# Graph-network layers on one Trainium2 core: sigmoid through tanh, attention scores spread through DRAM, first loads in another order

## The chip, the cores and the metric

The kernel runs on one core of a Trainium2 chip. The time is device time in microseconds (us), from one launch to its end. The profile has its own span, from the first to the last instruction, which is about 2 us shorter.

## What is computed

128 graphs of 128 nodes with 256 features each, and an adjacency matrix for every graph. Layer 0 is a gated graph network of three steps, layer 1 an attention over neighbours. Both work on a normalized input and add their result to `x`.

```python
def gru(inp, h):
    gi, gh = inp @ w_ih.T + b_ih, h @ w_hh.T + b_hh
    r, z = sigmoid(i_r + h_r), sigmoid(i_z + h_z)
    n = tanh(i_n + r * h_n)
    return (1 - z) * n + z * h
h = relu(layernorm(x))                       # layer 0
for i in range(3):
    m = h @ weight[i]
    aggr = einsum('bst,bsd->btd', A, m)      # A: adjacency as 0 and 1
    h = gru(aggr, h)
x = x + h
h = relu(layernorm(x))                       # layer 1
Wh = h @ W;  s = Wh.sum(-1)
e = leaky_relu(s[:, :, None] + s[:, None, :], 0.2)
alpha = softmax(where(adj == 0, -inf, e))
x = x + alpha @ Wh
```

## The kernel before

Four graphs make a group, so there are 32 groups. A group goes through three network steps (layers 0 to 2 in the code) and then through the attention. Three groups in different steps are worked on in turn, in an order that the list `turns` gives.

**The order of instructions.** The code does not issue its instructions as it goes. `op(engine, ns, fn, reads, writes, ...)` puts an operation on a list with an estimated duration, the buffers it uses and a due time. `Plan.run` then sorts all of them with these estimates and with a lag from one engine to the next, and issues them in that order; each engine, and SyncE (SP) for all transfers, works its own list off in sequence. An argument `two=True` tells the planner that a VectorE operation and a GpSimd operation can't run at once. So a changed estimate can change the order of everything. The matrix products of the gates carry due times of their own (`plan.cursor`), and form the chain around which the rest is placed.

**The gate products.** State and edge sums are multiplied with the two gate matrices in 2x2 blocks by seven products in place of eight, with sums and differences of blocks: `hs` (`node_sums` of the state, on GpSimd), `gs` (of the edge sums, on VectorE), `s_hh`, `s_x0` to `s_x2` (of the matrices, by `block_sums` at the start). The edge matrices `s_x` are compositions of `weight[i]` with `w_ih` (L431). `product` (L655, and L662 for the last step, which leaves its result with nodes on partitions) fills PSUM banks X, Y, Q for the gates r and z (`x_rz`, `y_rz`, `q_rz`) and for n (`x_n`, `y_n`, `q_n`). ScalarE copies X to Y (L702) and Y to `t2` and `t3` in SBUF (`put`, L692), VectorE adds Q (L695).

**The gates.** `gru` (steps 0 and 1) takes four blocks, from T3, X, Y and T2. For each it has the sigmoid of r and z on ScalarE (L740, L750), then on VectorE `(h_n + b) * r` (L743) and `+ i_n` (L747); for halves of the group it has tanh on ScalarE (L756) and three VectorE operations (L759 to L764) for `n + z * (h - n)`. `gru_rows` does the same for the last step (L778 to L804). The bias of n comes as a pointer to a column of `bias_h` in L743.

**Transposes.** Between node-wise and feature-wise layouts the data go through SP's transposing transfers, as 16-bit planes (`turned_halves`, `turned_parts`, `pl` to `plT`, L546). The edge sums (L597) multiply three bf16 parts of the state with the adjacency.

**Attention.** For a group: norm of `x1` to `h1`; `hw` (L868) gives the scores `s`, one number for each node; `turn_s` (L892) transposes the scores on TensorE into the PSUM bank `misc`, so that each partition has all 128 scores of a graph; the addition of these (L898) and of the own score (L899), leaky relu (L901), row maximum (L903), exponential (L910), sum (L912); transpose of the weights (`turned_weights`, L955, or by TensorE at L922 in the last two groups), weighted sum (L611), product with `W` (L935), and the addition to `x1` (L940), which is stored at L943. The exponential's estimate has 2570 ns more for loads of ScalarE's function table.

**Start.** SP's first entries in the kernel before are `w_ih` (768 KB, into `rz`), `x` of group 0, `w_hh` (768 KB), the message weights of layer 0, the adjacency, `x` of group 1, the two biases, `x` of group 2, the message weights of layer 1. `turned` (L344) transposes the gate weights on TensorE; the message weights follow at L418.

Of the kernel before, what the change touches and what calls it, by code (L numbers as in the profile page):

```python
# [23 lines left out]
MARGIN = 8000  # L24
GATES = 18150
# [185 lines left out]
def kernel(  # L211
# [31 lines left out]
    work = ctx.enter_context(tc.tile_pool(name="work", bufs=1))  # L243
    banks = ctx.enter_context(tc.tile_pool(name="banks", bufs=1, space=bass.MemoryType.PSUM))
# [25 lines left out]
        "hw": (1, "all", work, [P, D]), "e": (2, "all", work, [P, G, N]),  # L270
        "eT": (1, "all", work, [P, G, N]), "uT": (2, "all", work, [P, KD, GN]),
# [3 lines left out]
        "bias_s": (1, "all", const, [P, 3 * KD]),  # L275
# [37 lines left out]
    W = {t: buf(t) for t in ("s_hh", "s_x0", "s_x1", "s_x2", "bias_i", "bias_h", "bias_s", "seed_x",  # L313
# [12 lines left out]
    def load(dst, get, src, ns=100):  # L326
        op("SP", ns, lambda: nc.sync.dma_start(get(dst), src), [], [dst])
# [8 lines left out]
    def turned(src, dst, evict):  # L336

        for k in range(KD):
            for a in range(2):
                ps = bank()  # L340

                def turn(k=k, a=a, ps=ps):
                    for c in range(3):
                        nc.tensor.transpose(flat(ps)[:, c * P:(c + 1) * P],  # L344
                                            nat(src)[:, 3 * a + c, k * P:(k + 1) * P], ident)
                op("PE", 330, turn, [src], [ps])
                to_sbuf(evict[(2 * k + a) % len(evict)], 3 * P, ps, dst[k], 3 * P * a)
# [25 lines left out]
    def weights():  # L373
# [7 lines left out]
        def load_msg(layer):  # L381
            op("SP", 1300, lambda: nc.sync.dma_start(
                square(w_msg[layer]), weight[layer].rearrange("(k p) e -> p k e", p=P)),
               [], [w_msg[layer]])


        plan.due = -10 ** 6
        load(w_ih_nat, nat, w_ih.rearrange("(c p) e -> p c e", p=P), 4000)
        load_msg(0)
        plan.due = 10 ** 9  # L390
        load(w_hh_nat, nat, w_hh.rearrange("(c p) e -> p c e", p=P), 4000)
        load_msg(1)
        for t, src in (("bias_i", b_ih), ("bias_h", b_hh)):
            load(W[t], ap, src.rearrange("(c p) -> p c", p=P), 500)
        op("DVE", 170, lambda: nc.vector.tensor_add(ap(W["bias_s"]), ap(W["bias_i"]),
                                                    ap(W["bias_h"])),
           [W["bias_i"], W["bias_h"]], [W["bias_s"]])

# [44 lines left out]
        for t, i, b in ((tmp[0], 0, b_ih), (tmp[1], 0, b_hh), (tmp[2], 0, b_hh), (tmp[2], 1, b_ih)):  # L443
            n = t is tmp[2]
            op("SP", 500, lambda t=t, i=i, b=b, n=n: nc.sync.dma_start(
# [16 lines left out]
        load(W["w1"], ap, w_att.rearrange("(k p) e -> p k e", p=P), 1300)  # L462
# [209 lines left out]
    def products(layer, hT, hs, aT, gs, rows=False):  # L672
# [18 lines left out]
        def put(t, y):  # L691
            op("ACT", 590, lambda: nc.scalar.copy(ap(t), ap(y)), [y], [t])  # L692
# [4 lines left out]
        for kind, parts in kinds:  # L697
            X[kind], Y[kind] = buf("x_" + kind), buf("y_" + kind)
            if rows:
                seed(X[kind], kind, W["seed_x"])  # L700
            product(X[kind], 1, parts, not rows, rows=rows)
            op("ACT", 590, lambda x=X[kind], y=Y[kind]: nc.scalar.copy(ap(y), ap(x)),  # L702
               [X[kind]], [Y[kind]], mark=(plan.group, layer, kind))
# [5 lines left out]
        for kind, parts in kinds:  # L709
            product(Y[kind], 6, parts, False, rows=rows)  # L710
            T2[kind] = buf("t2_" + kind)
            put(T2[kind], Y[kind])
# [14 lines left out]
        return (1, 1, T3), (0, 0, X), y + (Y,), t2 + (T2,)  # L727

    def gru(layer, hT, hs, aT, gs):

        blocks = products(layer, hT, hs, aT, gs)
# [5 lines left out]
        for j, n, src in blocks:  # L737
# [3 lines left out]
                view(rz, 0)[:, j, n, :], ap(s_rz)[:, 0, :], AF.Sigmoid, bias=ap(W["bias_s"])[:, c:c + 1]),  # L741
               [s_rz, W["bias_s"]], [(rz, i, i + 1)])
            op("DVE", 480, lambda j=j, n=n, nn=nn, c=cn: nc.vector.scalar_tensor_tensor(  # L743
                view(u)[:, j, n, :], ap(nn)[:, 0, :], ap(W["bias_h"])[:, c:c + 1], view(rz, 0)[:, j, n, :],
                op0=OP.add, op1=OP.mult), [nn, (rz, i, i + 1), W["bias_h"]], [(u, i, i + 1)],
               two=nn.tag[0] == "t")
            op("DVE", 422, lambda j=j, n=n, nn=nn: nc.vector.tensor_tensor(  # L747
                view(u)[:, j, n, :], view(u)[:, j, n, :], ap(nn)[:, 1, :], OP.add),
               [nn], [(u, i, i + 1)], two=nn.tag[0] == "t")
            op("ACT", 500, lambda j=j, n=n, s_rz=s_rz, c=cz: nc.scalar.activation(  # L750
                view(rz, 1)[:, j, n, :], ap(s_rz)[:, 1, :], AF.Sigmoid, bias=ap(W["bias_s"])[:, c:c + 1]),
               [s_rz, W["bias_s"]], [(rz, 4 + i, 5 + i)])
        for j in (1, 0):
# [8 lines left out]
            op("DVE", 690, lambda d=d, cols=cols: nc.vector.tensor_tensor(  # L762
                ap(d), ap(d), ap(rz)[:, 1, cols], OP.mult), [(rz, 4 + lo, 4 + hi)], [d], two=True)
            op("DVE", 690, lambda j=j, d=d, cols=cols: nc.vector.tensor_tensor(  # L764
                ap(hT)[:, j, :], ap(u)[:, cols], ap(d), OP.add), [(u, lo, hi), d], [(hT, lo, hi)], two=True)

    def gru_rows(layer, hT, hs, aT, gs, rows, x1):

        blocks = products(layer, hT, hs, aT, gs, rows=True)
# [4 lines left out]
        for j, n, src in blocks:  # L774
# [5 lines left out]
                ap(s_rz).rearrange("p g (q m) -> p g q m", q=2), AF.Sigmoid),  # L780
               [s_rz], [(rz, i, i + 1), (rz, 4 + i, 5 + i)])
            op("DVE", 422, lambda outs=outs, graphs=graphs, nn=nn: nc.vector.tensor_tensor(
                view(u)[:, graphs, outs], ap(nn)[:, :, 0:P],
# [211 lines left out]
```

## Time and profile before

| | before |
|---|---|
| median of 3 runs | 2139.39 us (2138.39 to 2139.82) |
| the profiled execution | 2138.75 us, span 2136.9 us |
| TensorE matmul busy | 2108.1 us, 99% |
| VectorE busy | 1750.7 us, 82% |
| ScalarE busy | 1587.1 us, 74% |
| GpSimd busy | 951.0 us, 45% |
| transfers | 129.35 MB, queue busy 27.1% of 16 engines |

In lines of the profile, L12 is line 12 of the kernel before. PE is TensorE's matmuls, PEld its weight loads, DVE is VectorE, ACT is ScalarE, POOL is GpSimd, SPq is SyncE's queue. A group of instructions reads: line, engine, operation, output <- inputs, shapes, count, then busy us and mean ns of one, then idle time of the engine just before it and what ended that. A wait reads: who waited, for whom, us in total, times, longest. An engine that is busy less than the whole span costs time only where the engine that sets the end waits for it.

### The profile page before, as it was taken

Reading aid. Unit: us, or ns where it says so; the run is one execution under the profiler, and the core shown is the slowest. Engines: PE = TensorE matmul, PEld = TensorE weight load, DVE = VectorE, ACT = ScalarE, POOL = GpSimd, SP = SyncE. Lnnn points to the kernel's source line nnn. Section 1 sums busy time; section 2 is a strip of 40 time slices with the busy share of each in tenths; the row PEclk is TensorE's granted clock in tenths of the full one; section 3 lists DMA queues with packets and bytes.
Section 4 is the critical chain, followed back from the end, with each engine's and each line's share of the span. In section 5 each row is a group of like instructions: output and inputs, shape, how many; then the busy total and the mean of one; then the engine's idle time right before and its main releaser. Section 6 shows DMA issues by size and latency. Waiting matters only on the chain.

```text
span 2136.9 us, 33989 instructions
## 1 busy us (share of the span) xinstructions
PE 2108.1 (99%) x12550; PEld 1879.9 (88%) x12550; DVE 1750.7 (82%) x3297; ACT 1587.1 (74%) x2705; POOL 951.0 (45%) x889
## 2 busy tenths in 40 slices
PE   8999999999999999999999999999999999999997
PEld 7889888898888988889988889888888988988886
DVE  5677878788888889888898788888889888778777
ACT  5567877777877877777877777777777888676774
POOL 5545453445544445544344544355444454335421
PEclk9999999999999999999999999999999999999998
DMA  4222223232242312332222231313223323222221
GB/s 143 45 50 50 45 50 89 45 77 48 45 89 60 75 37 49 79 70 65 55 62 56 68 75 40 94 32 69 65 51 84 46 38 82 50 46 37 59 68 35
DMA packets 333430, 129.35 MB, mean 61 GB/s; under 512 B 264656, under 2 KB 333008, under 8 KB 333264
## 3 DMA queue, kind: packets, MB, share of 16 engines
q1 hardware_dynamic: 333264, 127.18, 27.1%
q8 instruction: 99, 1.62, 0.3%
q14 instruction: 67, 0.55, 0.1%
HBM read 45.36 MB, written 16.78 MB: 29 GB/s over the span
## 4 chain that ended last, share of the span: by engine, by line
PE 94%; DVE 3%; ACT 1%; DMA 1%; issue 1%; SPq 0%; DVEq 0%; ACTq 0%
PE y_rz L655 15%; PE q_rz L655 10%; PE x_rz L655 10%; PE y_rz L662 8%; PE y_n L655 7%; PE misc L597 6%; PE q_rz L662 5%; PE x_n L655 5%; PE x_rz L662 5%; PE q_n L655 5%; PE misc L935 5%; PE y_n L662 4%; PE misc L611 3%; PE x_n L662 3%; PE q_n L662 3%; PE misc L892 1%
## 5 line engine op out<-in xcount | busy, mean ns | idle before, releaser
L692 ACT COPY t_rz<-y_rz 128x512 f32<-128x512 f32 x192 | 112.3, 585 | 200.5 <-PE y_rz L662 104.9
L557 POOL TENSOR_TENSOR r<-rows 128x512 f32<-128x512 f32 x128 | 148.2, 1177 | 221.1 <-ACT rows L540 121.6
L625 POOL TENSOR_TENSOR hs<-hT 128x512 f32<-128x512 f32 x96 | 131.3, 1368 | 183.7 <-PE y_n L662 126.7
L655 PE MATMUL y_rz<-hs,s_hh 128*128 128x256 f32 x768 | 198.0, 380 | 2.6 <-ACT t_rz L692 2.6
L655 PE MATMUL y_rz<-gs,s_x 128*128 128x256 f32 x768 | 197.1, 379 | 0.0
L695 DVE TENSOR_TENSOR t_rz<-t_rz,q_rz 128x512 f32<-128x512 f32 x192 | 131.3, 684 | 69.4 <-PE q_rz L662 26.0
L582 POOL TENSOR_TENSOR pl<-d,pl 128x512 bf16<-128x512 f32 x64 | 77.9, 1219 | 217.8 <-ACT pl L580 217.7
L560 POOL TENSOR_TENSOR p<-r 128x512 bf16<-128x512 f32 x128 | 168.1, 1332 | 0.0
L655 PEld LDWEIGHTS y_rz<-gs,s_x 128*128 128x128 f32 x768 | 146.0, 190 | 19.8
L655 PEld LDWEIGHTS y_rz<-hs,s_hh 128*128 128x128 f32 x768 | 141.5, 190 | 21.8 <-ACT t_rz L692 4.0
L799 POOL TENSOR_TENSOR x<-x,u 128x512 f32<-128x512 f32 x64 | 88.1, 1379 | 143.0 <-ACT u L795 140.1
L695 DVE TENSOR_TENSOR t_n<-t_n,q_n 128x512 f32<-128x512 f32 x192 | 131.3, 684 | 22.5 <-ACT t_n L692 8.5
L629 POOL TENSOR_TENSOR hs<-hT,hs 128x256 f32<-128x256 f32 x96 | 74.1, 773 | 149.4 <-PE q_n L662 130.7
L577 POOL TENSOR_TENSOR d<-hT,pl 128x512 f32<-128x512 f32 x64 | 77.9, 1221 | 131.6 <-ACT pl L575 125.9
L692 ACT COPY t_n<-y_n 128x512 f32<-128x512 f32 x192 | 112.1, 584 | 29.5 <-PE y_n L655 16.8
L655 PE MATMUL x_rz<-hT,s_hh 128*128 128x256 f32 x512 | 131.5, 379 | 0.0
L655 PE MATMUL x_rz<-aT,s_x 128*128 128x256 f32 x512 | 131.5, 379 | 0.0
L935 PE MATMUL misc<-w,uT 128*128 128x256 f32 x512 | 121.7, 383 | 3.1 <-DVE e L898 1.7
L600 ACT COPY aT<-misc 128x512 f32<-128x512 f32 x192 | 110.6, 584 | 19.1 <-PE misc L597 13.7
L625 DVE TENSOR_TENSOR gs<-aT 128x512 f32<-128x512 f32 x96 | 96.8, 1009 | 27.4 <-ACT aT L600 27.4
L759 DVE TENSOR_TENSOR d<-hT,u 128x512 f32<-128x512 f32 x128 | 106.0, 828 | 12.2 <-ACT u L756 12.1
L655 PE MATMUL y_n<-hs,s_hh 128*128 128x256 f32 x384 | 114.5, 380 | 0.0
(215 smaller groups left out, 6548.9 us busy)
## 6 DMA issues: line engine op xcount, KB each, us to landing
rows<-in_x_dram SPq DMA_DIRECT2D x32, 512.0 KB, 4.2
x<-in_x_dram SPq DMA_DIRECT2D x32, 512.0 KB, 4.1
out_dram<-x SPq DMA_DIRECT2D x31, 512.0 KB, 3.0
at<-in_adj_dram SPq DMA_DIRECT2D x32, 256.0 KB, 2.8
plT<-pl SPq DMA_TRANSPOSE x186, 3.6
rz<-in_L_gnn_w_ih_dram SPq DMA_DIRECT2D x1, 768.0 KB, 5.0
rz<-in_L_gnn_w_hh_dram SPq DMA_DIRECT2D x1, 768.0 KB, 7.7
e<-in_L_gnn_weight_dram SPq DMA_DIRECT2D x3, 256.0 KB, 8.0
```

The lines of the kernel that those rows point to most:

```text
L557: op("POOL", 1106, lambda part=part: nc.gpsimd.tensor_tensor(ap(r1)[:, part], ap(rows)[:, part], top(rows)[:, part], OP.subtract), [(rows, ...
L560: op("POOL", 1050, lambda part=part: nc.gpsimd.tensor_tensor(ap(p3)[:, part], ap(r1)[:, part], top(r1)[:, part], OP.subtract), [(r1, n, n ...
L597: nc.tensor.matmul(flat(ps)[:, b * N:(b + 1) * N], part(i, b, k), ap(a)[:, b, :], start=(i == 0), stop=(i == 2))
L600: op("ACT", 590, lambda k=k, ps=ps: nc.scalar.copy(ap(dst)[:, k, :], flat(ps)), [ps], [(dst, 2 * k, 2 * k + 2)])
L625: op(eng, cost, lambda: sub(ap(w)[:, 0:2, :], blocks()[:, 1::2, :], blocks()[:, 0:2, :], OP.subtract), [t], [(w, 0, 2)], two=True)
L655: nc.tensor.matmul(ap(bank)[:, half, :], ap(w)[:, i - 1, q, :], source(t, sums), start=(first and c == 0 and m == 0), stop=False, skip_gro ...
L662: nc.tensor.matmul(ap(bank)[:, m, half * P:(half + len(chunk)) * P], source(t, sums)[:, m * N:(m + 1) * N], ap(w)[:, i - 1, q:q + len(chun ...
L692: op("ACT", 590, lambda: nc.scalar.copy(ap(t), ap(y)), [y], [t])
L695: op("DVE", 690, lambda: nc.vector.tensor_tensor(ap(t), ap(t), ap(q), OP.add), [q], [t])
L759: op("DVE", 690, lambda j=j, d=d, cols=cols: nc.vector.tensor_tensor(ap(d), ap(hT)[:, j, :], ap(u)[:, cols], OP.subtract), [(hT, lo, hi), ...
L799: op("POOL", 1290, lambda cols=cols, part=part: nc.gpsimd.tensor_tensor(part(x1), part(x1), ap(u)[:, cols], OP.add), [(u, lo, hi)], [(x1, ...
L935: nc.tensor.matmul(ap(ps)[:, b, :], ap(uT)[:, k, (m + b) * N:(m + b + 1) * N], ap(w1)[:, k, :], start=(k == 0), stop=(k == KD - 1))
```

## The change

1. `sigmoid(v)` is written as `(tanh(v / 2) + 1) / 2`. The activation becomes `Tanh` with scale 0.5 and a halved bias sum. The `+ 1` and the factor 0.5 go into the VectorE operations after it, which become scalar_tensor_tensor. For the block from X, which has r times a sum with a pointer bias, one more VectorE operation adds the 1. For the other blocks the bias of n is added by ScalarE when it copies: `put` copies in two halves, the first with a bias, for X to Y and for Y to T2 of kind n in steps 0 and 1. The exponential's estimate loses its 2570 ns.
2. For groups 0 to 29 the scores go to a DRAM tile `s_out` with one transfer (`128x4x1`, elements of 4 bytes) and come back with a second one that gives every partition all scores (`s_all`, 128x512). The planner takes 9500 and 5200 ns until they are there. The last two groups keep the transposes.
3. Loads get an estimate from their size (3 ns for a KB) and a lag of 3300 ns. `w_ih` is loaded in two halves; `turned` does the first half of rows first and waits for that half alone. The message weights of layers 0 and 1 get earlier due times. SP's first entries become: two halves of `w_ih`, message weights of layers 0 and 1, `x` of group 0, `w_hh`, adjacency, `x` of group 1, the biases, `x` of group 2.

```diff
+KB = 3
...
-    def load(dst, get, src, ns=100):
-        op("SP", ns, lambda: nc.sync.dma_start(get(dst), src), [], [dst])
+    def load(dst, get, src, kb):
+        op("SP", kb * KB, lambda: nc.sync.dma_start(get(dst), src), [], [dst], lag=3300)
...
-        for k in range(KD):
-            for a in range(2):
+        for a in range(2):
+            for k in range(KD):
...
-                op("PE", 330, turn, [src], [ps])
+                op("PE", 330, turn, [(src, a, a + 1)], [ps])
...
-        plan.due = -10 ** 6
-        load(w_ih_nat, nat, w_ih.rearrange("(c p) e -> p c e", p=P), 4000)
+        plan.due = -10 ** 9
+        for a in range(2):
+            part = slice(3 * a, 3 * a + 3)
+            op("SP", 384 * KB, lambda part=part: nc.sync.dma_start(
+                nat(w_ih_nat)[:, part], w_ih.rearrange("(c p) e -> p c e", p=P)[:, part]),
+               [], [(w_ih_nat, a, a + 1)], lag=3300)
         load_msg(0)
         plan.due = 10 ** 9
-        load(w_hh_nat, nat, w_hh.rearrange("(c p) e -> p c e", p=P), 4000)
+        load(w_hh_nat, nat, w_hh.rearrange("(c p) e -> p c e", p=P), 768)
+        plan.due = -10 ** 8
         load_msg(1)
+        plan.due = 10 ** 9
...
-        def put(t, y):
-            op("ACT", 590, lambda: nc.scalar.copy(ap(t), ap(y)), [y], [t])
+        def put(t, y, bias=None, mark=None):
+            if bias is None or rows:
+                op("ACT", 590, lambda: nc.scalar.copy(ap(t), ap(y)), [y], [t], mark=mark)
+                return
+            def halves():
+                nc.scalar.activation(ap(t)[:, 0], ap(y)[:, 0], AF.Identity,
+                                     bias=ap(W["bias_n"])[:, bias:bias + 1])
+                nc.scalar.copy(ap(t)[:, 1], ap(y)[:, 1])
+            op("ACT", 760, halves, [y, W["bias_n"]], [t], mark=mark)
...
-                view(rz, 0)[:, j, n, :], ap(s_rz)[:, 0, :], AF.Sigmoid, bias=ap(W["bias_s"])[:, c:c + 1]),
-               [s_rz, W["bias_s"]], [(rz, i, i + 1)])
+                view(rz, 0)[:, j, n, :], ap(s_rz)[:, 0, :], AF.Tanh, bias=ap(W["bias_s"])[:, c:c + 1],
+                scale=0.5), [s_rz, W["bias_s"]], [(rz, i, i + 1)])
+            if src is X:
+                op("DVE", 290, lambda j=j, n=n: nc.vector.tensor_scalar(
+                    view(rz, 0)[:, j, n, :], view(rz, 0)[:, j, n, :], 1.0, None, op0=OP.add),
+                   [], [(rz, i, i + 1)])
...
+            else:
+                op("DVE", 480, lambda j=j, n=n, nn=nn: nc.vector.scalar_tensor_tensor(
+                    view(u)[:, j, n, :], view(rz, 0)[:, j, n, :], 1.0, ap(nn)[:, 0, :],
+                    op0=OP.add, op1=OP.mult), [nn, (rz, i, i + 1)], [(u, i, i + 1)],
+                   two=nn.tag[0] == "t")
...
+        if g < NG - 2:
+            s_out, s_all = buf("s_out"), buf("s_all")
+            def spread():
+                return ap(s_all)
+            op("SP", 100, lambda: nc.sync.dma_start(ap(s_out).rearrange("g n -> n g"), ap(s)),
+               [s], [s_out], lag=9500)
+            op("SP", 100, lambda: nc.sync.dma_start(
+                ap(s_all), ap(s_out).rearrange("(o g) n -> o g n", o=1).to_broadcast([P, G, N])),
+               [s_out], [s_all], lag=5200)
+        else:
+            s_all = buf("misc")
...
-        op("ACT", 2570 * (g < NG - 1) + 320 * n, exps, [low], [e], turn=(g + 2, 1, "rz"))
+        op("ACT", 320 * n, exps, [low], [e], turn=(g + 2, 1, "rz"))
```

In the changed kernel the transpose of the scores stands at L939, the score addition at L945, the exponential at L958, `plT` at L561, `w_ih`'s halves at L391 and the other loads at L330.

## Prediction

> **What bounds the kernel now.** I read the page first: the busy shares and the chain that ended last.
>
> ```profile
> span 2136.9 us, 33989 instructions
> ...
> PE 2108.1 (99%) x12550; PEld 1879.9 (88%) x12550; DVE 1750.7 (82%) x3297; ACT 1587.1 (74%) x2705; POOL 951.0 (45%) x889
> ...
> PEclk9999999999999999999999999999999999999998
> ...
> PE 94%; DVE 3%; ACT 1%; DMA 1%; issue 1%; SPq 0%; DVEq 0%; ACTq 0%
> ```
>
> TensorE has work in 2108 of 2137 us and is 94% of the chain. A busy PE can still be a slow PE, so I asked the trace how far apart matmuls start. In the middle, eight f32 matmuls of 256 columns take 1.73 us (0.216 each) wherever the chain is followed. It is a dense stream. Next, the stages, for where the missing 28.8 us lie (columns: length, then busy us of PE, PEld, DVE, ACT and POOL with counts, clock, DMA share, GB/s):
>
> ```profile
> 0.00:25.00 25.00, 20.10 (x108) 15.35 (x108) 10.66 (x41) 8.90 (x18) 13.98 (x21) 0.93 0.77 221
> 25.00:50.00 25.00, 22.50 (x129) 19.33 (x130) 18.79 (x38) 19.50 (x39) 14.74 (x15) 0.93 0.27 85
> ...
> 200.00:2000.00 1800.00, 1795.01 (x10778) 1609.45 (x10776) 1517.58 (x2831) 1381.20 (x2334) 810.36 (x746) 1.00 0.28 60
> ...
> 2100.00:2120.00 20.00, 12.10 (x52) 9.50 (x51) 17.27 (x41) 7.19 (x14) 4.10 (x6) 0.74 0.08 26
> 2120.00:2137.00 17.00, 10.55 (x46) 7.72 (x44) 7.47 (x24) 3.85 (x11) 0.00 (x0) 0.90 0.19 63
> ```
>
> PE is idle 7.4 us in the first 50, 5.0 in the long middle and 14.4 in the last 37. So in the middle only a PE instruction that goes is time won. The waits of PE name what ended the idle stretches:
>
> ```profile
> PE misc L922 <- DVE x L940: 5.6, 2, 5.1
> PE y_rz L655 <- ACT t_rz L692: 2.6, 3, 1.4
> PE misc L344 <- DMA rz<-in_L_gnn_w_hh_dram: 2.3, 1, 2.3
> ...
> PE misc L344 <- DMA rz<-in_L_gnn_w_ih_dram: 1.0, 1, 1.0
> ```
>
> The last two are first loads (2.3 us for `w_hh`, 1.0 for `w_ih`), the first is the attention of the last group, the second is ScalarE being late.
>
> **What the Trainium skill says.** "ScalarE: Activation LUTs", section "What ACT_TABLE_LOAD costs", gives 1283 ns for a load and more for a drain; section "Table sets: the hidden batching unit" has exp and tanh in one set, sigmoid in another. The trace agrees: 63 loads of 1283 ns, at the exponentials and at the sigmoid after them. "SBUF — State Buffer", section "SBUF: two separate sides", says that a VectorE operation with two SBUF inputs and a GpSimd operation that reads SBUF exclude each other on a shared port. L899 below agrees: 692 ns in the median, 1653 at worst. "DMA: Bandwidth & Descriptors", section "Two DMAs through the same engine are not ordered", has the issuing engine wait for the first transfer's semaphore before it issues a dependent one: that is the new wait on SP. No transfer of the kernel before shows it for a store and its reload.
>
> **The change, part by part.** The sum is made against the profiled span, 2136.9 us, whose execution took 2138.75; the three runs have their median at 2139.39.
>
> *Scores by way of DRAM.* For groups 0 to 29 the four transposes of `turn_s` (L892) go: 120 of 128.
>
> ```profile
> L892 PE MATMUL misc<-ident,s 128*128 128x128 f32 x128 | 20.3, 275 | 0.7 <-DVE x L940 0.7
> ```
>
> and in the timeline:
>
> ```profile
> 2067.97 0.60 PE L892 MATMUL misc<-ident,s 128*128 128x128 f32 x4
> 2068.41 1.03 PE L662 MATMUL y_rz<-s_x,gs 128*128 128x256 f32 x4
> ```
>
> 275 ns is the latency of one; four keep the next matmul away for 2068.41 - 2067.97 = 0.44 us, 0.11 each. 120 x 0.11 = 13.2 us, all of it on the path. This is the surest term; the two ends are 12 and 19 (20.3 x 120/128, the busy time).
> In their place SP issues a 4-byte-element store `s_out` and a broadcast load `s_all` for each group. Nearest rows (KB, us to landing):
>
> ```profile
> e<-in_L_gnn_b_ih_dram SPq DMA_DIRECT2D x1, 256.0 KB, 3.5
> ...
> bias_i<-in_L_gnn_b_ih_dram SPq DMA_DIRECT2D x1, 3.0 KB, 7.6
> ```
>
> The store has 512 elements against 768 of `bias_i`, which landed amid the first loads, so 4 to 8 us; the reload 3.5. Their issues took 1.4 to 2.2 us and 0.5 in the timeline: 30 pairs, some 60 to 80 us of SP, which otherwise mostly sits at a wait. The scores arrive about 10 us later than by PE. Who waits? In the trace of a middle group (g = 14) the scores end at 1103.8, the exponentials run at 1110.5, and `eT`, ready at 1123.4, is first multiplied at 1134.1: 10.7 us of slack there, and other groups have 4 to 20. The planner is told of both delays, too. So nothing on PE. But behind the waiting `s_all` in SP's order stand the two `plT` transposes of a `turned_halves` (8x128), which `rows` or `hT` and then the edge products wait for. In the steady part two to four other SP entries come between `s_out` and `s_all`, among them the out store, the `plT` transpose of 12x128 and the reload of `x1`, which waits for the out store: the score store has mostly landed by then. On VectorE the score addition (L945) now waits for `s_all`. In the order it stands 19 instructions behind the last `hw`; at some 0.65 us each and an engine 82% busy that is about 15 us, and the two transfers with SP's waits between them need 10 to 15. Where it is late, the node sum of `gs` behind it (L644, used by the fourth product alone) and the gates wait too; in 65 us a group VectorE has 11 of slack. Nothing here stands in GpSimd's queue. I take 0.5 us for SP and VectorE together, between 0 and 4; the bad end is the first rival.
>
> *Tanh for sigmoid.* The order of the changed kernel has 1 table load for 63: 62 x 1.283 = 79.5 us of ScalarE. Against it, `put` splits into two halves 128 times: a half with a bias pointer like L740 (473 ns from PSUM) and a 256-column copy like L351 (366), 839 for 585, so 128 x 0.25 = 33. ScalarE goes from 1587 to about 1541. Its gain reaches PE only where ScalarE was late. That is the wait for `t_rz` at 227.6 (1.35 us), which has table loads at 218.6 and 224.6 ahead of it, perhaps also one or two more late ones; I take 1.5 us of the middle's 5.0, between 0 and 3. In the last stage the load at 2102.4 lay inside a wait for VectorE's `low`: nothing.
> On VectorE tensor_tensor becomes scalar_tensor_tensor. Does that cost?
>
> ```profile
> L899 DVE TENSOR_TENSOR e<-e,s x33: 426/692/1653, 216.0 to 2123.4; 128x512 f32<-128x512 f32 x31, 128x256 f32<-128x256 f32 x2
> ...
> L901 DVE SCALAR_TENSOR_TENSOR e<-e x33: 424/692/1530, 216.8 to 2123.9; 128x512 f32<-128x512 f32 x31, 128x256 f32<-128x256 f32 x2
> ...
> L747 DVE TENSOR_TENSOR u<-u,x_n x64: 420/421/422, 43.5 to 2021.7; 128x256 f32<-128x256 f32 x64
> ...
> L743 DVE SCALAR_TENSOR_TENSOR u<-x_n,bias_h,rz x64: 470/483/486, 42.9 to 2021.2; 128x256 f32<-128x256 f32 x64
> ```
>
> With a number as scalar, no (692 and 692); with a pointer, 62 ns. So the exchanges cost 0, and 192 L743 without pointer save 12 us. The new `+1` on the X block, 64 times, has no row: "VectorE: DVE Perf Modes", section "The perf-mode tier table", gives an f32 scalar operation in SBUF twice the rate, from which I estimate 290 ns; the 256-column copy from PSUM (425) is the upper end: 19 to 27 us. The score addition reads SBUF instead of PSUM: 687 to 692 alone, with the port shared up to 920 (L899's mean), 0 to 7. VectorE: +7 to +22, to 83% or 84%. Neither engine becomes the bound; the extra latency in a gate chain (0.3 us) lies under other groups' products.
>
> *First loads.* `w_ih` comes in two halves, `turned` takes the first half first, both message weights pass ahead of `x`, and `w_hh` moves from third to behind `x`. In the trace, 768 KB had landed at 5.8 us and `w_hh`, with 2048 KB issued, at 9.6: 1280 KB in 3.8 us, 340 KB per us. Half of `w_ih` is there 384/340 = 1.1 us earlier: the wait of 1.0 goes. `w_hh` now has 2560 KB before its end: about 11.1 us. By then PE has, from 4.7 on, the four `w_ih` turns (1.5 us in the timeline), four of the messages (1) and three compositions (4.3): busy until 11.5, so the wait of 2.3 goes as well. Against it: `x` of group 0 lands 1.5 us later (8.8), and its norm, GpSimd's `r1` and `p3` and the edge products shift; the remaining compositions (5 us), now ahead of these, hide it. The second message may be waited for, 0.5. SP's later entries (adjacency, biases) keep their sequence and are needed later. Start: -3.0, between -6.5 and +2. The 2.7 us of idle at 25 to 28 us I leave as they are.
>
> *Tail.* The last two groups keep their transposes, and the late idle is a chain of VectorE, ScalarE and PE with the same operations: 0, between -3 and +4, since the order is planned anew. Group 29's scores come 10 us later where `eT` had 1.5 us of slack; the planner puts its products later among those of the last group.
>
> Sum: -13.2 - 1.5 - 3.0 + 0.5 (SP and VectorE) = -17.2 us. 2136.9 becomes 2119.7, and the median 2139.4 becomes 2122.
>
> **Rivals.**
> - *SP's queue blocks (slower).* The 4-byte store lands later than the plan has it, `s_all` stands at the head of SP, the `plT` transposes behind it and VectorE's L945 come late, and PE waits at the edge products or for `gs`. Against: PE waited 0.2 us in all for `plT` in the whole trace. For: SP is the only queue and nearly always at a wait, and L945 has little to spare. It decides from 17.2/30 = 0.57 us per group on; at 0.9 each it gives 2122 + 27 = 2149.
> - *Small new waits eat a part.* The start gives nothing, and the new order in middle and tail costs 4 to 5 us: -13.2 + 4.5, 2130.5.
> - *VectorE through the port.* The `+1` and the added SBUF reader hold GpSimd up (`hs`, `r1`), and PE waits some 0.2 us in each of 64 gate blocks, 13 us: 2135 to 2139, no change.
> - *More is won.* The middle's waits vanish (3.5 more) and the tail loses the 5 us at L922: 2114.
> - *No single table after all.* Excluded: the order shows one load.
>
> **How the numbers follow.** Forecast 0.49, with 2117 to 2127 as its own range; small waits 0.18; more won 0.15; port 0.07; SP 0.11. Faster by over 0.2% (4.3 us, about what a measurement of this kernel can tell from no change) are the first three, 0.82; same 0.07; slower 0.11. The range 2113 to 2134 holds these three but for their ends.
>
> **What would show it.** After: 8 matmuls of the score transpose, PE busy about 2093, its share still 99%; one table load, ScalarE near 1540; VectorE 1758 to 1773; no PE wait for `w_hh`. A `w_hh` wait, or PE idle in the middle above 8 us with `plT` or `rows` as releaser, would make me wrong; so would `s_out` landings above 10 us with SP waiting for them and PE behind.

## The result, and the profile after

The changed kernel took 2156.11 us (median, 2155.08 to 2157.05) against 2139.61 us (2138.39 to 2140.66) of the kernel before on the same chip: ratio 1.0077, 95% interval 1.006 to 1.0095. It is slower by 0.8%, clear of the scatter, and outside the range of the prediction. From the page of the kernel after:

```profile
span 2154.3 us, 33935 instructions
...
PE 2102.5 (98%) x12430; PEld 1864.9 (87%) x12430; DVE 1721.6 (80%) x3364; ACT 1525.9 (71%) x2771; POOL 936.5 (43%) x889
...
PEclk9999999999999999999999999999999999999998
...
PE 72%; DMA 12%; DVE 12%; ACT 3%; issue 1%; SPq 0%; POOL 0%; DVEq 0%; ACTq 0%; POOLq 0%
```

The 120 matmuls are gone and every engine is busy for less time than before, at the same clock; yet the span is 17.4 us longer. In the chain that ended last, transfers hold 12% where they held 1%. The stages of the kernel after, with the columns of before:

```profile
0.00:25.00 25.00, 20.54 (x116) 15.67 (x116) 15.22 (x42) 12.15 (x25) 11.91 (x17) 1.00 0.89 253
25.00:50.00 25.00, 24.05 (x139) 19.90 (x138) 18.15 (x44) 16.33 (x35) 18.02 (x21) 1.00 0.18 54
200.00:2000.00 1800.00, 1771.06 (x10557) 1578.46 (x10556) 1466.29 (x2840) 1308.99 (x2363) 792.77 (x743) 1.00 0.36 63
```

The start got denser (44.6 us busy of 50, before 42.6). The long middle, where PE had 5.0 us of idle time, now has 28.9. PE's waits name the places:

```profile
PE misc L612 <- DMA plT<-pl: 20.2, 25, 2.2
PE y_n L670 <- ACT t_n L715: 8.3, 23, 0.5
PE misc L970 <- DVE x L988: 3.7, 1, 3.7
...
PE misc L433 <- DMA e<-in_L_gnn_weight_dram: 1.5, 1, 1.5
```

25 times PE stands at the edge products for a transposing transfer (0.2 us in all before), 23 times at the seventh product for ScalarE's copy of kind n. To make the account I add up how much later than back to back each matmul starts (216 ns for 256 f32 columns, 110 for 128, 56 for bf16). Such idle time was 48.8 us before and is 79.2 after: -5.1 in the first 50 us, +1.3 up to 200, +32.4 from 200 to 2000, +1.9 behind. With 13.2 us less of work the 30.4 us more make +17.2; the spans differ by 17.4.

Why is `plT` late? The score store (L929), its min, median and max in us from issue to landing:

```profile
L929 SPq DMA_DIRECT2D s_out<-s x30: 359/371/377, 199.0 to 2083.2; - x30
...
DMA to landing us min/median/max: 8.2/10.5/10.9
```

and the out store and the transposing transfers in the list of transfers (KB, then us to landing; before 3.0 and 3.6):

```profile
out_dram<-x SPq DMA_DIRECT2D x31, 512.0 KB, 6.9
...
plT<-pl SPq DMA_TRANSPOSE x186, 4.1
```

One group of the middle in the timeline of SP's queue (start, us, line, transfer):

```profile
981.98 0.37 SPq L929 DMA_DIRECT2D s_out<-s  x1
986.81 0.38 SPq L991 DMA_DIRECT2D out_dram<-x  x1
987.36 1.90 SPq L561 DMA_TRANSPOSE plT<-pl  x1
993.42 0.38 SPq L330 DMA_DIRECT2D x<-in_x_dram  x1
993.85 0.51 SPq L931 DMA_DIRECT2D s_all<-s_out  x1
```

`plT` is issued 5.4 us behind the score store and nothing holds its issue. But by the trace's semaphore times the score store lands at 992.23, the out store at 993.36 and `plT` at 994.68, and the edge products that need it start at 994.82. So it is the landing that is late, 7.3 us after the issue. What the transfer engines did meanwhile (columns as in the stages; the last two are DMA share and GB/s):

```profile
983.40:986.80 3.40, 3.40 (x19) 3.01 (x18) 3.35 (x7) 0.59 (x2) 0.00 (x0) 1.00 0.00 0
986.80:990.00 3.20, 3.20 (x24) 2.99 (x23) 2.27 (x4) 2.26 (x4) 2.00 (x2) 1.00 0.96 146
990.00:992.20 2.20, 2.20 (x15) 1.99 (x14) 0.91 (x3) 0.20 (x1) 0.00 (x0) 1.00 1.22 28
992.20:993.40 1.20, 1.20 (x10) 1.12 (x10) 0.42 (x1) 1.20 (x2) 0.00 (x0) 1.00 0.69 157
```

The score store's own packets are all through 1.3 us after its issue, and the transfer engines then stand empty (0 GB/s) although it has not landed. The out store and `plT` start, fall to 28 GB/s, and run at 157 once the score store has landed: 1266 of the 1536 packets of `plT` start after that. So the data of `plT` are held, and not only the report of its landing.

Over the whole trace, 52 transfers were issued while a score store was under way, and none of them landed before it: the out stores 1.3 us behind it in the median, the transposing ones 2.7.

PE wants `plT` about 12.2 us after the score store's issue and gets it 2.5 us after its landing; the wait per group is then about the landing less 9.7 us. That gives 25 x 0.8 = 20 us here; it fits below for the kernels that keep this store on SP's queue and this order.

### The profile page after: what moved, and what is told of

Its sections match the earlier page's. It is cut to its first block, busy times and chain, and to the rows that moved or that the text cites. A ratio compares the mean times of both kernels' runs of the same rounds, so it can differ in the third digit from the quotient of the medians.

```text
span 2154.3 us, 33935 instructions
## 1 busy us (share of the span) xinstructions
PE 2102.5 (98%) x12430; PEld 1864.9 (87%) x12430; DVE 1721.6 (80%) x3364; ACT 1525.9 (71%) x2771; POOL 936.5 (43%) x889
## 4 chain that ended last, share of the span: by engine, by line
PE 72%; DMA 12%; DVE 12%; ACT 3%; issue 1%; SPq 0%; POOL 0%; DVEq 0%; ACTq 0%; POOLq 0%
PE y_rz L670 12%; DMA plT<-pl 9%; PE q_rz L670 8%; PE x_rz L670 8%; PE y_n L670 7%; PE y_rz L677 5%; PE misc L612 5%; PE x_n L670 4%; PE q_n L670 4%; PE q_rz L677 4%; PE x_rz L677 3%; PE misc L983 3%; PE misc L626 3%; PE q_n L677 2%; PE y_n L677 2%; PE x_n L677 2%
## 5 line engine op out<-in xcount | busy, mean ns | idle before, releaser
L572 POOL TENSOR_TENSOR r<-rows 128x512 f32<-128x512 f32 x128 | 138.3, 1101 | 325.7 <-ACT rows L555 161.1
L640 POOL TENSOR_TENSOR hs<-hT 128x512 f32<-128x512 f32 x96 | 126.9, 1322 | 163.6 <-PE y_n L677 103.7
L670 PEld LDWEIGHTS y_rz<-gs,s_x 128*128 128x128 f32 x768 | 145.9, 190 | 19.8
L575 POOL TENSOR_TENSOR p<-r 128x512 bf16<-128x512 f32 x128 | 157.4, 1249 | 0.0
L640 DVE TENSOR_TENSOR gs<-aT 128x512 f32<-128x512 f32 x96 | 108.3, 1128 | 55.2 <-ACT aT L615 55.2
L836 POOL TENSOR_TENSOR x<-x,u 128x512 f32<-128x512 f32 x64 | 97.0, 1518 | 49.4 <-ACT u L832 45.8
L795 DVE SCALAR_TENSOR_TENSOR d<-rz,d 128x512 f32<-128x512 f32 x128 | 114.5, 894 | 1.7
L670 PE MATMUL y_n<-gs,s_x 128*128 128x256 f32 x384 | 114.3, 379 | 0.0
```

Of the source, the lines that this page charges most:

```text
L572: op("POOL", 1106, lambda part=part: nc.gpsimd.tensor_tensor(ap(r1)[:, part], ap(rows)[:, part], top(rows)[:, part], OP.subtract), [(rows, ...
L575: op("POOL", 1050, lambda part=part: nc.gpsimd.tensor_tensor(ap(p3)[:, part], ap(r1)[:, part], top(r1)[:, part], OP.subtract), [(r1, n, n ...
L640: op(eng, cost, lambda: sub(ap(w)[:, 0:2, :], blocks()[:, 1::2, :], blocks()[:, 0:2, :], OP.subtract), [t], [(w, 0, 2)], two=True)
L670: nc.tensor.matmul(ap(bank)[:, half, :], ap(w)[:, i - 1, q, :], source(t, sums), start=(first and c == 0 and m == 0), stop=False, skip_gro ...
L795: op("DVE", 690, lambda d=d, cols=cols: nc.vector.scalar_tensor_tensor(ap(d), ap(rz)[:, 1, cols], 1.0, ap(d), op0=OP.add, op1=OP.mult), [( ...
L836: op("POOL", 1290, lambda cols=cols, part=part: nc.gpsimd.tensor_tensor(part(x1), part(x1), ap(u)[:, cols], OP.add), [(u, lo, hi)], [(x1, ...
```

## The experiments

Theory A: the store of 4-byte elements lands late and holds up the transfers behind it. Theory B, the first rival of the prediction: SP stands at the reload's wait, and `plT` is issued late. Theory C: the copies of kind n in two halves make ScalarE late at the seventh product. Ratios are against the kernel before, run on the same chip; the series of experiments had different chips.

**Another layout of the scores** (the whole change, but `s_out` is node by node, so an element has 16 bytes; every engine has the same instructions in the same order):

```diff
-        "s_all": (1, "all", work, [P, G, N]), "s_out": (2, "all", dram, [G, N]),
+        "s_all": (1, "all", work, [P, N, G]), "s_out": (2, "all", dram, [N, G]),
...
-            op("SP", 100, lambda: nc.sync.dma_start(ap(s_out).rearrange("g n -> n g"), ap(s)),
+            op("SP", 100, lambda: nc.sync.dma_start(ap(s_out), ap(s)),
```

> The changed kernel with the scores stored node by node: 128 elements of 16 bytes in place of 512 of 4, the order of all engines as in the changed kernel. Theory A (the store of 4-byte elements holds the transfer engines for some 10 us, and the transposing transfer issued behind it lands late): the store lands in 2 to 4 us, PE's wait for plT falls from 20 us to under 4, time 2156 - 18 = about 2138. Theory C (the split copies on ScalarE hold up PE): the wait of PE for t_n stays at 8 us. If neither the store's size nor its duration matters (theory B, SP stands at the wait for the reload), the time stays within 3 us of 2156.

2132.13 us, ratio 0.9968 (0.9957 to 0.998). Its store, and the top of PE's waits:

```profile
L929 SPq DMA_DIRECT2D s_out<-s x30: 332/339/348, 197.6 to 2057.7; - x30
...
DMA to landing us min/median/max: 1.4/1.7/3.4
```

```profile
PE y_n L670 <- ACT t_n L715: 7.7, 23, 0.3
PE misc L970 <- DVE x L988: 3.4, 1, 3.4
```

The store lands in 1.7 us instead of 10.5 and all waits for `plT` go. PE idles 24 us less between 200 and 2000, 20 of them at `plT`. This alone turns the sign. The reload has the other layout too; that it is the store, and not the reload, is shown further down, where the store alone is changed. The 23 waits for ScalarE stay.

**The reload left out** (a constant is added instead of the scores of the other nodes; the 4-byte store stays):

```diff
-            op("SP", 100, lambda: nc.sync.dma_start(
-                ap(s_all), ap(s_out).rearrange("(o g) n -> o g n", o=1).to_broadcast([P, G, N])),
-               [s_out], [s_all], lag=5200)
+            op("SP", 100, lambda: None, [s_out], [s_all], lag=5200)
```

> The changed kernel with the 4-byte store as it is, but the reload of the scores left out; the score addition reads a constant tile instead, so the scores of other nodes are missing from the attention of groups 0 to 29. The planned order is the same but for this entry. Theory A (the store holds the transfer engines): no gain, 2153 to 2157, PE still waits about 20 us for plT. Theory B (SP's queue stands at the reload's wait, and the transposing transfers behind it come late; or the 256 KB of the reload are in the way): PE's wait for plT falls under 6 us, time about 2138.

2210.94 us, 1.0352 (1.0329 to 1.0374). PE's first wait:

```profile
PE misc L613 <- DMA plT<-pl: 54.8, 26, 3.3
```

SP has no reload to stand at, and PE waits for `plT` all the same, more than ever. Theory B falls. By the semaphore times the store took 11.8 us here in the median, and the relation above gives 26 x 2.1 = 55 us. The time missed my 2153 to 2157 by far: of the 53 us that this span is longer than that of the changed kernel, 35 are at `plT`, and most of the others come from a lower clock, which is shown below with the store on ScalarE's queue.

**The copies of kind n in one piece** (the bias of n in the copies left out):

```diff
-                nc.scalar.activation(ap(t)[:, 0], ap(y)[:, 0], AF.Identity,
-                                     bias=ap(W["bias_n"])[:, bias:bias + 1])
-                nc.scalar.copy(ap(t)[:, 1], ap(y)[:, 1])
+                nc.scalar.copy(ap(t), ap(y))
```

> The changed kernel with the copies X to Y and Y to T2 of kind n in one piece again (the bias of n from these copies is left out), planned with the same estimate, so in the same order. Theory C (the split copy, 0.25 us longer, keeps PE from product 7 in bank y_n): PE's wait for t_n, 8 us in 23 waits, goes, and with some 0.4 to 0.5 us for each of 32 rounds the time falls by 8 to 13 us, to about 2146. Theory A alone: no change, 2156, the wait only moves to plT.

2205.49 us, 1.0312 (1.0297 to 1.0327): slower, with 55.8 us of waits for `plT` and a store of 11.7 us. That one instruction less for ScalarE slows a store seemed unlikely, so I set the same edit beside the changed kernel itself:

> The changed kernel with the copies of kind n in one piece (their bias of n left out), beside the changed kernel itself in the same call. Its first run had 2205 us with the store landing after 11.8 us. If that landing belonged to that run and not to this kernel, it is now like the control's and the time 1 to 4 us below the control; if the kernel itself makes the store slow, it is again 2200 or so.

> The changed kernel once more, as the control for the next run. PE's wait for plT is 25 to 26 waits of (landing of the store + 2.5 - 12.2 us): 20 us at 10.5, 28 at 10.8. Time 2150 to 2170 on the two landings seen; a landing of 11.8 would give about 2195.

2172.35 us (1.0156) against 2177.79 (1.0178), both with a store of 11.2 us and 38.8 us of waits for `plT`. The one piece is worth some 5 us, and the store's landing differs between series of runs: 10.5, 10.8, 11.2 and 11.7 us, with 20.2, 28.4, 38.8 and 55.8 us of waits (the relation gives 20, 28, 39 and 52). The changed kernel's time goes with it:

> The changed kernel unaltered, beside others of this call. In its first profile the 4-byte store landed in 10.5 us and PE waited 20 us for plT; in the two runs with the store kept (no reload, no split) it took about 11.8 us and PE waited 55 us. Theory A (the transposing transfer issued 5.4 us behind the store lands some 2.5 us after it, and PE needs it 12.2 us after the store's issue): PE's wait is 30 groups times (landing + 2.5 - 12.2), so whatever the landing is here, 10.5 gives 2156 and 11.8 about 2195. A time near 2156 with a landing near 11.8 would speak against A.

2163.88 us, 1.0115 (1.0099 to 1.0132), and later once more 2178.86, 1.0179. Why a series has one landing and not another is open; the chip changed with the series and may be the reason, which no run here separates. With the other layout, the piece alone:

> The changed kernel with the scores stored node by node (16-byte elements) and the copies of kind n in one piece (their bias of n left out), planned with the same estimates. Theory C: the remaining waits of PE for t_n (7.7 us in 23 waits with node-wise storing) go, and with them 8 to 13 us: 2132 - 10 = about 2122. If the split copies cost nothing, 2132.

2129.94 us, 0.9962 (0.9947 to 0.9977). PE still waits 23 times at that place, 4.5 us instead of 7.7. The halves explain 3 us; theory C falls for the rest.

**Each part alone.** The first keeps the scores on TensorE, with tanh and the loads as changed:

```diff
-        if g < NG - 2:
+        if False:
```

> The changed kernel with the scores of all groups transposed on TensorE, as before; tanh and first loads as changed. PE has 120 transposes more, 13 us. Theory A: the wait for plT (20 us) goes, so 2156 + 13 - 20 = about 2149; the wait for t_n stays. If the store and reload were free, it would be 2156 + 13 = 2169.

2125.68 us, 0.9946 (0.9931 to 0.9961), 23 us better than the 2149 of theory A, which had taken away the `plT` waits alone. No `plT` and no repeated `t_n` waits are left; idle time is 39.4 us where the changed kernel has 79.2 and the kernel before 48.8. So with the way through DRAM the changed kernel idles 40 us more, and not only the 20 us at `plT`.

The next three are the kernel before with one item of the change each; the core of each edit:

```diff
-                view(rz, 0)[:, j, n, :], ap(s_rz)[:, 0, :], AF.Sigmoid, bias=ap(W["bias_s"])[:, c:c + 1]),
+                view(rz, 0)[:, j, n, :], ap(s_rz)[:, 0, :], AF.Tanh, bias=ap(W["bias_s"])[:, c:c + 1],
+                scale=0.5), [s_rz, W["bias_s"]], [(rz, i, i + 1)])
```

> The kernel before with the tanh part alone (scores by TensorE, loads as before). PE's work is that of before. With both tanh and loads and TensorE's scores it was 2125.7, 13 below before. If the loads give 4, tanh gives some 5 to 9: 2131 to 2135. If the table loads were wholly hidden and the split copies cost PE time, 2140 or more.

Tanh alone: 2130.89 us, 0.9962 (0.9947 to 0.9977); idle time from 200 to 2000 is 9.4 us for 14.8 before.

```diff
-        load(w_ih_nat, nat, w_ih.rearrange("(c p) e -> p c e", p=P), 4000)
+        for a in range(2):
+            part = slice(3 * a, 3 * a + 3)
```

> The kernel before with the first loads' part alone. The prediction has -3.0 us for it; in the changed kernel PE's idle in the first 50 us is some 5 us less than before. So about 2135; 2139 if the wait is only moved.

The loads alone: 2138.77 us, 1.0 (0.9992 to 1.0009). Idle time in the first 50 us falls from 12.7 to 6.5, and part of it comes back later:

```profile
PE y_rz L661 <- ACT t_rz L698: 4.4, 4, 1.5
...
PE q_rz L668 <- DVE gs L631: 3.2, 1, 3.2
```

```diff
+            op("SP", 100, lambda: nc.sync.dma_start(ap(s_out).rearrange("g n -> n g"), ap(s)),
+               [s], [s_out], lag=9500)
```

> The kernel before with the DRAM way of the scores alone (4-byte store, sigmoid and loads as before). Theory A: PE has 13 us less work but waits for plT behind the store, 20 us and more if the store lands later than 10.5 us, and some order effects: 2145 to 2165. If the loss of the changed kernel came from its parts together and not from the store, 2127.

The scores by way of DRAM alone: 2167.47 us, 1.0129 (1.0114 to 1.0144). Its store lands in 9.5 us, but the waits are at another place than theory A had them:

```profile
PE y_rz L657 <- ACT t_rz L694: 22.6, 20, 3.2
```

This loss is mostly not the one of the changed kernel. Of the 20 waits, 17 end 45 to 56 us after the latest score store was issued, when it has long landed, and ahead of eight of them ScalarE had just stopped for VectorE's `u`. So I put them down to the planned order, which no run here tests. In both orders the loss belongs to the scores by way of DRAM; the two other parts are a gain of 13 us together (2125.68 against 2138.96 beside it).

**What makes the store slow, and how it holds others.** In two kernels based on the one without the reload, a constant again takes the place of the scores. One stores only the first graph's 128 elements, side by side; the other stores all 512, but 64 bytes apart (`s_out` is [G, N, 16]).

```diff
-            op("SP", 100, lambda: nc.sync.dma_start(ap(s_out).rearrange("g n -> n g"), ap(s)),
+            op("SP", 100, lambda: nc.sync.dma_start(ap(s_out)[0:1].rearrange("g n -> n g"), ap(s)[:, 0:1]),
```

```diff
-            op("SP", 100, lambda: nc.sync.dma_start(ap(s_out).rearrange("g n -> n g"), ap(s)),
+            op("SP", 100, lambda: nc.sync.dma_start(ap(s_out)[:, :, 0:1].rearrange("g n o -> n g o"),
+                                                    ap(s).rearrange("p (g o) -> p g o", o=1)),
```

> Leaves out the reload of the scores and the scores of three of a group's four graphs: each group stores 128 elements of 4 bytes instead of 512, to the same lines of DRAM, and a constant is added in place of the scores. If the landing grows with the number of 4-byte elements (fixed 1.5 us plus 9 us for 512), the store lands in 3 to 5 us, the transposing transfers of the adjacency come in time and TensorE has no wait at the edges (time 2128 to 2138). If the size of one element alone or a fixed cost of a 4-byte write sets it, the store stays above 9 us and the kernel above 2150.

> Leaves out the reload of the scores, and a constant is added in place of the scores: each group stores its 512 elements of 4 bytes 64 bytes apart in DRAM instead of side by side. If several 4-byte writes into one line of DRAM hold each other up, the store lands in 2 to 5 us and TensorE's waits at the edges go (2128 to 2138). If each element costs what it costs wherever it goes, the landing stays at 10 to 12 us, the kernel at 2150 to 2210 as with the reload left out alone.

2131.61 us, 0.9956 (0.9936 to 0.9975), and 2130.91, 0.9956 (0.9937 to 0.9976). The store of the first, then of the second:

```profile
L930 SPq DMA_DIRECT2D s_out<-s x30: 333/343/839, 192.4 to 2055.8; - x30
...
DMA to landing us min/median/max: 7.4/7.8/11.0
```

```profile
L930 SPq DMA_DIRECT2D s_out<-s x30: 360/372/375, 198.8 to 2057.8; - x30
...
DMA to landing us min/median/max: 1.8/1.9/2.7
```

The first lies between what the two theories gave: a quarter of the elements still takes 7.8 us. The second decides: all 512, spread out, take 1.9. So neither the number of elements nor their size is slow by itself; 4-byte writes side by side are. In both layouts of 512 the store's packets are through 1.3 us after the issue, so the rest of the slow landing passes after the transfer engines have sent them. In both kernels the waits for `plT` are gone, and the time is that of the 16-byte layout. Since the reload is left out in both, and in the slow kernel beside them, the store's layout alone makes this difference. "DMA: Bandwidth & Descriptors", section "Specifications", says that a transfer below 512 B is done as read-modify-write. The trace agrees for the slow store if such writes wait for each other at one place, but by that sentence the spread store and the 16-byte one would be slow too, and they are fast. The mechanism remains an inference.

The store from ScalarE's queue instead of SP's, at the same place of the order:

```diff
-            op("SP", 100, lambda: nc.sync.dma_start(ap(s_out).rearrange("g n -> n g"), ap(s)),
+            op("SP", 100, lambda: nc.scalar.dma_start(ap(s_out).rearrange("g n -> n g"), ap(s)),
```

> The changed kernel with the 4-byte store issued by ScalarE on its own queue at the same place of the order, everything else as it is. If the transposing transfers are late because they stand behind the store in SP's queue, they land 4 to 5 us after their issue and TensorE's waits at the edges go (2130 to 2140). If it is the transfer engines that the store holds, whoever issued it, the transposing transfers still land 7 to 8 us after their issue and the edges still wait for 20 to 50 us in all (2150 to 2200).

> The changed kernel again, as the control of this call: the store lands in 10.5 to 11.8 us, TensorE waits 20 to 55 us in all at the edges by the same relation as before, time 2155 to 2205.

2203.66 us, 1.0294 (1.0264 to 1.0324), the control 2178.86, 1.0179 (1.0149 to 1.0208), two runs each. PE's first wait with the store on ScalarE's queue:

```profile
PE misc L612 <- DMA plT<-pl: 51.8, 24, 2.8
```

`plT`, on SP's queue, still lands 2.5 us in the median behind a store on another queue that took 11.2 us. The order of the landings thus agrees with the same page, section "Queues, rings and completion order": the semaphore increment of a transfer lands only after every earlier write of that transfer engine, across its queues. By itself that would only make the report late. The 28 GB/s above show more: the data behind the store wait too. What holds them is open.

Of the 25 us to the control, 11.5 are at `plT`. Most of the others are a lower clock. The clock granted to TensorE (0.988 in the mean, 0.997 in the control) is the column before the last two:

```profile
939.20:942.60 3.40, 1.09 (x15) 0.78 (x15) 0.49 (x2) 0.22 (x1) 0.00 (x0) 1.00 0.64 138
942.60:946.00 3.40, 3.40 (x18) 3.04 (x19) 0.12 (x1) 2.57 (x4) 0.00 (x0) 0.50 1.05 263
946.00:949.40 3.40, 3.40 (x21) 3.10 (x20) 3.01 (x4) 1.20 (x2) 1.96 (x2) 0.99 0.99 261
```

After a wait of 2.3 us for `plT` the clock is halved for 3.4 us. Between 60 and 2060 us this happens nine times, and never in the control's trace. Half of 3.4 us nine times is an estimate of 15 us. The kernel without the reload has fifteen such stretches (an estimate of 26 us), the first run of the copies in one piece twelve, the changed kernel at the top of this document none. In the traces of the kernels that wait for `plT` there are 40 such stretches. Each begins during a pause of about 2.1 us or more between two matmul starts, or within 1.4 us after it; not every such pause brings one. By this estimate a wait that brings one costs 1.7 us more than its length.

**The other wait.** Theory D: ScalarE's copy into `t2_n` (L713) overwrites a buffer of which there is one, and has to wait for VectorE's last reader (L822) of the old content. From the groups by line of the kernel after (busy us, mean ns, then idle before it and until whom):

```profile
L713 ACT ACTIVATE t_n<-y_n,bias_n 128x256 f32<-128x256 f32 x64 | 29.9, 467 | 56.5 <-DVE u L822 52.7 <-PE y_n L670 3.5 <-DVE st L495 0.3
```

In VectorE's order the planner has put the scores' five operations (L945 to L953) and a norm's statistics ahead of that reader, since it was told that the scores take 9500 + 5200 ns to arrive. If so, another figure moves them:

```diff
-            op("SP", 100, lambda: nc.sync.dma_start(ap(s_out), ap(s)),
-               [s], [s_out], lag=9500)
+            op("SP", 100, lambda: nc.sync.dma_start(ap(s_out), ap(s)),
+               [s], [s_out], lag=3000)
```

> The changed kernel with node-wise storing (16-byte elements) and with the planner told of 3000 ns for the store in place of 9500 (measured 2 us), so that VectorE's score addition and its maximum stand ahead of the gates' last Q additions and no longer between these and the reads of t2_n. Theory D (the split is not the cause of PE's wait for t_n: ScalarE's copy into t2_n waits until VectorE has read the old t2_n, and the score operations stand before that read): the t_n waits go, 2132 - 12 = about 2120. If the order on VectorE plays no part, 2132.

2122.26 us (2121.67 to 2123.74), 0.9921 (0.9906 to 0.9935), the fastest of all. Its page, the top of PE's waits, and the copy into `t2_n`:

```profile
PE 2093.4 (99%) x12430; PEld 1867.0 (88%) x12430; DVE 1750.3 (82%) x3364; ACT 1534.4 (72%) x2771; POOL 935.3 (44%) x889
```

```profile
PE misc L939 <- DVE x L988: 5.3, 1, 5.3
PE misc L970 <- ACT e L958: 3.7, 1, 3.7
```

```profile
L713 ACT ACTIVATE t_n<-y_n,bias_n 128x256 f32<-128x256 f32 x64 | 30.4, 474 | 14.8 <-PE y_n L670 14.8
```

Both repeated waits are gone, and the copy no longer waits for VectorE at all. From 200 to 2000 PE idles 9.5 us, against 22.9 with the planner told 9500. Theory D holds, with one reservation: the new figure moves other operations as well. What is left is the tail: 27.5 us idle behind 2000 us, where all scores on TensorE had 20.0. Are the late scores of the last group that goes by way of DRAM the cause?

```diff
-        if g < NG - 2:
+        if g < NG - 3:
```

> The kernel with scores stored node by node and 3000 ns told for the store, but with the last three groups instead of the last two keeping the score transposes on TensorE. If the 7.5 us that TensorE idles more in its tail than with all scores on TensorE come from group 29's late scores, the tail's idle time falls from 27.5 to 20 to 23 us and the time to 2116 to 2120. If the tail is a matter of the order alone, it stays within 2 us of 2122.

> Tanh and the loads with all scores transposed on TensorE, again, beside the kernel with scores by way of DRAM in one call. By PE's idle times the DRAM path with 16-byte elements is worth 13.2 us less 7.5 us of tail, so this one should be 5 to 6 us slower than the 2122 of that kernel with two groups kept, at 2125 to 2129.

2128.76 us, 0.9948 (0.9929 to 0.9968), and 2127.86, 0.9943 (0.9923 to 0.9962). The tail falls to 19.8 us as expected, but the time does not: the new order brings 22 waits of its own in the middle.

```profile
PE misc L626 <- ACT aT L615: 7.1, 22, 0.8
```

So the tail's 7.5 us seem to come from there, as far as a changed order can show it, and the 13.2 us taken off TensorE are worth some 5 us against all scores on TensorE (0.9921 against 0.9946 and 0.9943, in other series of runs, with intervals that overlap or touch). That this gain is real was not settled.

## Why the prediction was wrong

The sign was wrong, and the step that failed is the landing of the store: "The store has 512 elements against 768 of `bias_i`, which landed amid the first loads, so 4 to 8 us". `bias_i` reads 4-byte elements from DRAM; the store writes them, side by side. It took 10.5 to 11.8 us in the runs of this order. The second half of the error followed: "the score store has mostly landed by then", and "I take 0.5 us for SP and VectorE together, between 0 and 4". I looked only at whether the issue of `plT` would be held, and did not ask whether its landing could be. The term measured 20 us at `plT` and 8 at ScalarE's copy (theory D), about 28 for 0.5. The prediction gave landings above 10 us, with SP waiting for them and PE behind, as what would make it wrong. The landings and PE's waits came; that SP stood at them did not, but for five times.

- *First rival, SP's queue blocks (2149, chance 0.11).* Right in sign, in place (`plT`, edge products) and nearly in size. Wrong in the mechanism: SP waited for the store at L931 only five times, leaving the reload out took no wait away, and `plT` was issued in time.
- *120 transposes, -13.2.* Right. PE busy was foretold as about 2093 us; where no repeated wait is left it is 2093.4. In the changed kernel the same matmuls count as 2102.5 us, so busy time also takes in waiting: a busy PE is not a dense PE.
- *Tanh, -1.5 (0 to 3).* Too small. Alone it gave 2130.89 against 2139.29, -8.4 us. Of this, 5.4 us of idle time went between 200 and 2000: the three waits for `t_rz` (2.6 us), of which I had counted one, and single waits for other operations. Another 2.1 went in the first 50 us and 1.0 behind 2000, where I had put nothing. Its pieces were right: one table load, the halves 467 + 364 = 831 ns (839 foretold), ScalarE at 1525.9 to 1536.5 us (1541).
- *First loads, -3.0.* The start's idle time fell by 5.1 us in the changed kernel, the `w_hh` wait is gone. By themselves the loads were worth nothing in the time: later waits took most of it back.
- *VectorE, +7 to +22.* Wrong in sign, without effect on the time: 1721.6 for 1750.7 us. The added 1 took 294 ns in the median, as estimated (290); the mean of 397 comes from nine of 64 that took 724 to 1379 ns beside a running GpSimd instruction. But the operations that share a port with GpSimd met it less often. The addition of a node's own score (L899 before, L947 now) fell from 952 to 692 ns for 512 columns: before, 13 of 31 took over 750 ns, all of them beside a running GpSimd instruction; now none does, and one of 31 has GpSimd beside it. The order alone moves VectorE as far: the same instructions took 1722.8 us with the 16-byte layout and 1750.3 with the other figure for the planner.
- *Tail, 0 (-3 to +4).* +1.9 us of idle time behind 2000 in the changed kernel, inside; +7.3 (27.5 for 20.2) in the fastest one, outside. The reason foretold, group 29's late scores, is the one that the last experiment points to.

The sum of the forecast, 2122, is what the same change gives with a 16-byte element and a truthful delay for the planner: 2122.26. That is partly chance: tanh alone gained 7 us more than foretold and the tail lost 7.3.

## What to carry to other kernels

Before moving data by way of DRAM, ask how its elements lie at the destination and what is issued behind the store: here a store of 2 KB delayed every transfer issued while it was out, from the same queue and from another, so the wait appeared at an innocent transfer. Take the price of a store from a store with the same layout, not from a load. And the delay that a planner is told is part of the kernel: with a figure that was about true for the slow store, the fast one lost 10 us to the order alone.

## What was not expected of the hardware

- 512 writes of 4 bytes side by side in DRAM landed in 9.5 to 11.8 us in the median of a run, 128 of them in 7.8; the same 512 spread 64 bytes apart in 1.9, and 128 of 16 bytes side by side in 1.4 to 1.7.
- Of 52 transfers issued while such a store was out, none landed before it. In the median the transposing one right behind an out store took 7.7 us, where it took 4.6 with 16-byte elements; an out store took 6.9 where 3.0 was.
- Such a store was sent in 1.3 us; then nothing moved until the next transfers began, and these fell to 28 GB/s until it had landed.
- Behind waits of a little over 2 us the granted clock was halved for 3.4 us at a time, nine to fifteen times in the kernels whose store took 11.2 to 11.8 us with 52 to 56 us of waits, but not in the control with the same 11.2 us and 40 us of waits.
- The same store in the same program landed in 10.5, 10.8 and twice in 11.2 us in four series of runs, the later three on three chips; the changed kernel took 2156, 2164, 2178 and 2179 us. The cause is open.
